# A four-layer graph network on one core: the preparation and the end of the hyperbolic layers rewritten in a fixed order

## Chip, core and metric

The kernel runs on one core of a Trainium2 chip. The metric is the device time of one execution in microseconds. Times of single instructions come from one profiled execution. The engines are TensorE (PE), VectorE (DVE), ScalarE (ACT), GpSimd (POOL) and SyncE (SP); SP issues nearly all large transfers, ScalarE and GpSimd issue some small ones from their own queues.

## What is computed

`x` is 3327 x 64, `adj` is a 3327 x 3327 matrix of zeros and ones with about 0.5% ones. Four layers follow each other; each normalizes its rows, applies a ReLU and adds its result to `x`:

```python
h = jnp.maximum(_layernorm(x, axis=-1), 0.0);  x = x + _L0_gnn_ref(h, adj, ...)   # hyperbolic attention, c = 1
h = jnp.maximum(_layernorm(x, axis=-1), 0.0);  x = x + _L1_gnn_ref(h, adj, ...)   # sum over the last 100 neighbours with decay
h = jnp.maximum(_layernorm(x, axis=-1), 0.0);  x = x + _L2_gnn_ref(h, adj, adj, ...)   # two GRU cells
h = jnp.maximum(_layernorm(x, axis=-1), 0.0);  x = x + _L3_gnn_ref(h, adj, ...)   # hyperbolic attention, c = 1 / r**2
```

The change concerns layers 0 and 3. Both compute, for all pairs of rows,

```python
adj_att = sigmoid(left + right.T) * adj            # left, right: products of logmap0(h) with two weight columns
x_local = _logmap(h[:, None, :], h[None, :, :], C)
support_t = einsum('ij,ijd->id', adj_att, x_local)
return _proj(_expmap(h, support_t, C), C)
```

Here `h` is the normalized row after the ReLU, called h' below; its squared length |h'|^2 enters nearly every factor.

## The kernel before

Rows are padded to 3328 = 26 tiles of 128. `X` holds all of x in SBUF as 128 partitions x 26 tiles x 64 numbers. A function `hyperbolic_series` does a hyperbolic layer; it is called for layer 0 (`r` is None, `masks` is None: adj is read from memory as f32) and for layer 3 (`masks` holds adj as fp8 in SBUF, and `done` stores each finished half). It has three stages.

**Preparation** (L361 to L479). `norm_relu` makes the means, `H`, its squares on ScalarE, their sums on VectorE, a root with one refinement step (`sqrt_`, L95 to L103), and writes the normalized rows back to `H`. Then H is squared and summed again for `x2` = |h'|^2. From `x2` come `ax` = x2 - 1, its inverse `ia`, and `Xr` = H x 2 ia. `Xr` is split into two f16 parts, `hi` and `lo`, in `Xp`. TensorE transposes Xp to columns (`to_columns16`, L410; the copies out of PSUM alternate between ScalarE and VectorE), multiplies these with the weights (`pw`), and VectorE makes `left` and `right` from that. `left` is brought to one row per tile, `LT`, and spread over the partitions as `leftB` by matmuls (L461). `Xe` holds the f16 rows with nine extra columns (from x0 = (x2 + 1) ia, split in three), is transposed to `XE`, and the first chunk's part to `XF`. `keep_busy` issues matmuls whose result is not used (L423). Here Tile's scheduler orders the instructions of each engine.

**Loop** (L482 to L630). The columns are cut in four chunks of 4, 3, 3 and 3 tiles per half. For each of 4 x 26 pairs of chunk and row tile: ScalarE makes `sig` (L517), POOL multiplies it with adj (L519), TensorE makes the products in a PSUM slot (L530, L531), ScalarE squares (`y`, L537), VectorE applies the series and multiplies with `sig` (L542, L543), TensorE sums (L552, L560). The order is written by hand. `load(k)` (L503) fetches adj for layer 0 into four buffers; its first four calls stand at the start of the loop, in the pool of the loop. The loop leaves `M`, `M0`, `hm` and `mm`.

**End** (L632 to L742). Some seventy VectorE instructions on 128 x 26 numbers, mostly each waiting for the one before, with Sqrt and Tanh on ScalarE, give two factors `ah` and `am` per row; then X gets Xr x ah + M x am (L739, L740), in halves in layer 3, in one piece in layer 0.

In layer 1, which follows the end of layer 0, ScalarE loads the weights `wt` (L1251, L1252) after POOL has cleared that tile (L1250); POOL issues the loads of other weights (L1213 to L1226) ahead of it. VectorE's first step of that layer is the mask (L1287).

Of the kernel before, what the change touches and what calls it, by code (L numbers as in the profile page):

```python
# [19 lines left out]
P = 128  # L20
# [26 lines left out]
def tile_gnn4(ctx: ExitStack, tc: tile.TileContext, x, adjT, att0, b0, w1, bias1, w_gat, a_gat,  # L47
# [46 lines left out]
    def sqrt_(pool, src, name):  # L94

        s0 = pool.tile(list(src.shape), F32, name=name)
        rc = pool.tile(list(src.shape), F32, name=name + "_r")
        A.activation(s0, src, AF.Sqrt)
        V.reciprocal(rc, s0)
        V.tensor_mul(rc, rc, src)  # L100
        V.tensor_add(s0, s0, rc)
        V.tensor_scalar(s0, s0, 0.5, None, op0=OP.mult)
        return s0  # L103
# [200 lines left out]
    def hyperbolic_series(r, params, ok, masks=None, done=None):  # L304
# [18 lines left out]
        with ExitStack() as st:  # L323
# [18 lines left out]
            px = st.enter_context(tc.tile_pool(name="hsx", bufs=2))  # L342
            XC, XF, leftB = {}, {}, {}
# [20 lines left out]
            with tc.tile_pool(name="hsp", bufs=1) as tp, tc.tile_pool(name="hsps", bufs=2, space=PSUM) as ps:  # L364
                A.memzero(X0)
                Xe = tp.tile([P, T, KE + 9], F16, name="Xe")
                E, Fe = Xe[:, :, D:KE], Xe[:, :, KE:]
                V.memset(E[:, :, 6:], SX)
                for k, part in enumerate(f16_parts((1.0 - 2.0 * G1) * SX)):
                    V.memset(Fe[:, :, 6 + k:7 + k], part)  # L370

                def parts3(x_, name, dtype):

                    o = tp.tile([P, T, 3], dtype, name=name)
                    lo = tp.tile([P, T], F32, name=name + "_r")
                    for k in range(3):
                        V.tensor_copy(o[:, :, k], x_ if k == 0 else lo)
                        if k < 2:
                            V.tensor_sub(lo, x_ if k == 0 else lo, o[:, :, k])
                    return o  # L380

                H = tp.tile([P, T, D], F32, name="H")
                norm_relu(tp, H)
                sq = tp.tile([P, T, D], F32, name="sq")
                for ts in HALVES:
                    A.activation(sq[:, ts, :], H[:, ts, :], AF.Square)
                for ts in HALVES:
                    V.reduce_sum(x2[:, ts], sq[:, ts, :], axis=AX.X)
                if r is not None:
                    V.tensor_scalar(x2, x2, cc, None, op0=OP.mult)  # L390
                ax = tp.tile([P, T], F32, name="ax")
                V.tensor_scalar(ax, x2, 1.0, None, op0=OP.subtract)
                V.reciprocal(ia, ax)
                ia2 = tp.tile([P, T], F32, name="ia2")
                V.tensor_scalar(ia2, ia, 2.0, None, op0=OP.mult)
                if r is not None:
                    V.tensor_scalar(ia2, ia2, sqc, None, op0=OP.mult)
                for ts in HALVES:
                    V.tensor_mul(Xr[:, ts, :], H[:, ts, :], wide(ia2[:, ts]))
                    A.activation(hi[:, ts, :], Xr[:, ts, :], AF.Copy, scale=SX)  # L400
                V.tensor_scalar(root, x2, 1.0, None, op0=OP.max)
                root_ = sqrt_(tp, root, "zs")
                table_of(AF.Sigmoid, root_[:, :1])
# [3 lines left out]
                def to_columns16(dst, src, rows, odd):  # L407
                    for t0 in range(0, T, 4):
# [6 lines left out]
                        else:  # L415
                            A.activation(dst[:, t0 * P:(t0 + n) * P], pt[:rows, :n * P], AF.Copy)

                junk = ps.tile([P, 512], F32, name="junk", bufs=1)
# [7 lines left out]
                to_columns16(XT, Xp[:, :, :2 * D], P, 1)  # L426
# [6 lines left out]
                A.activation(Xe[:, :, :D], Xr, AF.Copy, scale=SX)  # L433
                x0 = tp.tile([P, T], F32, name="x0")
                V.scalar_tensor_tensor(x0, x2, 1.0, ia, op0=OP.add, op1=OP.mult)
                x0s = tp.tile([P, T], F32, name="x0s")
                V.tensor_scalar(x0s, x0, SX, None, op0=OP.mult)
                p0 = parts3(x0s, "p0", F16)
                h0, hm0, m0, l0 = p0[:, :, 0:1], p0[:, :, 0:2], p0[:, :, 1:2], p0[:, :, 2:3]
                for k, src in ((0, h0.to_broadcast([P, T, 3])), (3, m0.to_broadcast([P, T, 2])), (5, l0)):  # L440
                    V.tensor_copy(E[:, :, k:k + src.shape[-1]], src)


                V.tensor_copy(root, root_)
                z = tp.tile([P, T], F32, name="z")
                V.reciprocal(z, root)
                V.tensor_mul(z, z, ax)
                V.tensor_scalar(z, z, 0.5 * ARTANH_CLIP / SX, isqc, op0=OP.mult, op1=OP.mult)
                lr = tp.tile([P, T, 2], F32, name="lr")
                V.reduce_sum(lr, pw[:, :6 * T].rearrange("p (t k i) -> p t k i", k=2, i=3), axis=AX.X)  # L450
                left = tp.tile([P, T], F32, name="left")
                V.tensor_mul(left, lr[:, :, 0], z)
                pe = ps.tile([P, W], F32, name="pe", bufs=1)
                PE.transpose(pe[:T, :P], left, ident)
                A.activation(LT, pe[:T, :P], AF.Copy)
                nc.sync.dma_start(left_row, LT)
                c = chunks[0]
                for o, to in ((0, junk), (1, pe)):
                    for i in range(c[1]):
                        t = o * HT + c[0] + i  # L460
                        PE.matmul(to[:, i * P:(i + 1) * P], ident[:T, t:t + 1].to_broadcast([T, P]), LT,  # L461
                                  start=True, stop=True)
                    A.activation(leftB[c][:, o, :], to[:, :c[1] * P], AF.Copy)
# [1105 lines left out]
```

## Time and profile before

| | us |
|---|---|
| median of 3 runs (lowest to highest) | 829.16 (827.92 to 830.69) |
| profiled execution | 831.17 |
| its span, first to last instruction | 829.5 |
| VectorE busy in the span | 721.5 (87%) |
| TensorE busy | 662.2 (80%) |
| ScalarE busy | 562.0 (68%) |
| POOL busy | 419.0 (51%) |

The layers lie in the span so: preparation of layer 0 to about 31 us, its loop to 266, its end to 284; layers 1 and 2 to 543; preparation of layer 3 to 569, its loop to 802, its end to 822, and the last store after that. A row of the timeline gives start, duration, engine, line, operation and tiles, and in brackets the idle time of the engine before it with what ended it. A row of the chain gives start and duration of a piece of the chain of work that ended last. A queue that issues transfers is written ACTq or SPq.

### The profile page before, as it was taken

To read this page: it belongs to the slowest core of one execution; us is meant where nothing else is said; L and a number is where in the kernel's file an instruction comes from. 1 tells how busy PE (TensorE), PEld (TensorE's weight loads), DVE (VectorE), ACT (ScalarE), POOL (GpSimd) and SP (SyncE) were. 2 spreads that over 40 slices of the span, in tenths; PEclk is the share of its full clock that TensorE was granted. 3 is DMA by queue.
4 is the path that set the end of the run, shared out by engine and by line. 5 is a ranking of instruction groups with operands and counts; after the bars stand their busy time and mean duration, and the time that the engine had idled before them with its cause. 6 is when DMAs were issued, how large, how long until landed. Compare 5 with 4: busy or idle time off the path is not lost.

```text
span 829.5 us, 11810 instructions
## 1 busy us (share of the span) xinstructions
PE 662.2 (80%) x4228; PEld 251.2 (30%) x4228; DVE 721.5 (87%) x1013; ACT 562.0 (68%) x684; POOL 419.0 (51%) x283
## 2 busy tenths in 40 slices
PE   0889999999896059989970997618999999998940
PEld 0422233333331024435430662204222333333310
DVE  7689999999997999999989946796999999999966
ACT  3878888888884167777761306448888888888850
POOL 2499989989985310002300000004787777787720
PEclk9999999999999569999995899958999999999985
DMA  2577766767662639999943630002001001000001
GB/s 42 167 235 227 204 204 191 238 182 204 190 191 66 225 126 339 349 347 333 338 170 126 220 113 1 0 0 48 1 2 35 1 1 35 0 2 1 0 4 44
DMA packets 56887, 107.86 MB, mean 130 GB/s; under 512 B 8305, under 2 KB 32817, under 8 KB 56817
## 3 DMA queue, kind: packets, MB, share of 16 engines
q1 hardware_dynamic: 51712, 106.68, 40.2%
q10 hardware_dynamic: 4656, 0.08, 0.3%
q8 instruction: 35, 0.57, 0.3%
q0 software_dynamic: 448, 0.24, 0.1%
q14 instruction: 36, 0.29, 0.1%
HBM read 103.73 MB, written 0.88 MB: 126 GB/s over the span
## 4 chain that ended last, share of the span: by engine, by line
DVE 65%; PE 14%; DMA 7%; ACT 6%; issue 5%; POOL 2%; ACTq 1%; DVEq 0%; POOLq 0%
DVE sig L543 22%; DVE slot L542 20%; DMA adj<-in 7%; DVE same L1207 5%; PE acc L1407 5%; DVE mask L1287 3%; POOL sig L519 2%; PE slot L552 2%; ACT y L537 1%; DVE deg L1426 1%; PE cnt L1294 1%; DVE X L740 1%; DVE prod L739 1%; PE slot L560 1%; DVE ln_v L123 1%
## 5 line engine op out<-in xcount | busy, mean ns | idle before, releaser
L537 ACT ACTIVATE y<-slot,shift_c 128x768 f32<-128x768 f32 (+1 forms) x208 | 197.6, 950 | 69.7 <-ACT sig L517 48.1
L543 DVE TENSOR_TENSOR sig<-slot,sig 128x768 f32<-128x768 f32 (+1 forms) x208 | 213.2, 1025 | 24.7 <-POOL sig L519 2.7
L542 DVE SCALAR_TENSOR_TENSOR slot<-y,slot 128x768 f32<-128x768 f32 (+1 forms) x208 | 212.1, 1020 | 9.0 <-ACT y L537 8.9
L519 POOL TENSOR_TENSOR sig<-adj,sig 128x768 f32<-128x768 f32 (+1 forms) x104 | 201.8, 1962 | 24.8 <-ACT sig L517 14.7
L517 ACT ACTIVATE sig<-leftB,right 128x768 f32<-128x768 f32 (+1 forms) x208 | 204.1, 981 | 0.2
L519 POOL TENSOR_TENSOR sig<-mask,sig 128x768 f32<-128x768 fp8e4 (+1 forms) x104 | 174.6, 1680 | 57.2 <-ACT sig L517 53.1
L552 PE MATMUL slot<-sig,Xr 128*64 128x384 f32 (+1 forms) x832 | 187.2, 538 | 18.3 <-DVE sig L543 18.3
L530 PE MATMUL slot<-XC,XT 128*128 128x384 f16 (+1 forms) x416 | 142.1, 342 | 5.0 <-DVE sig L543 3.3
L531 PE MATMUL slot<-XF,XE 73*128 73x384 f16 (+1 forms) x416 | 141.4, 340 | 0.0
L1300 ACT ACTIVATE w<-cnt,ebias 128x832 bf16<-128x832 f32 x104 | 93.8, 950 | 32.4 <-PE cnt L1294 32.4
L1207 DVE TENSOR_SCALAR_CACHE_REDUCE same<-adj 128x1664 bf16<-128x1664 f32 x52 | 97.7, 1880 | 3.5 <-DMA adj<-in 3.5
L560 PE MATMUL slot<-sig,X 128*32 128x384 f32 (+1 forms) x832 | 95.0, 529 | 0.0
L468 POOL COPY Xp<-Xe 128x234 f16<-128x234 f16 x2 | 0.8, 415 | 160.1 <-DVE XT L414 146.4
L552 PEld LDWEIGHTS slot<-sig,Xr 128*64 128x64 f32 x832 | 42.9, 135 | 123.9 <-DVE sig L543 85.2
L1294 PE MATMUL cnt<-mask,after 128*128 128x416 fp8e4 x208 | 54.8, 347 | 25.3 <-DVE mask L1287 22.6
L178 POOL TENSOR_TENSOR mask<-mask,offdiag 128x128 fp8e4<-128x128 fp8e4 x26 | 16.8, 666 | 105.4 <-PE cnt L1294 104.2
L530 PEld LDWEIGHTS <-XT 128*128 128x128 f16 x416 | 40.6, 98 | 94.7 <-issue 68.8
L1294 PE MATMUL cnt<-mask,rest 128*128 128x416 fp8e4 x208 | 55.0, 347 | 12.5 <-ACT w L1300 12.5
L1287 DVE TENSOR_SCALAR mask<-adj 128x1664 fp8e4<-128x1664 f32 x52 | 53.3, 1031 | 6.7 <-DMA adj<-in 6.6
L531 PEld LDWEIGHTS <-XE 73*128 73x128 f16 x416 | 40.7, 98 | 33.3 <-issue 9.3
L1311 PE MATMUL acc<-w,h 128*64 128x416 bf16 x416 | 47.2, 349 | 0.0
L1407 PE MATMUL acc<-mask,h 128*64 128x416 fp8e4 x416 | 38.3, 346 | 0.1
(293 smaller groups left out, 547.7 us busy)
## 6 DMA issues: line engine op xcount, KB each, us to landing
adj<-in SPq DMA_DIRECT2D x65, 832.0 KB, 6.9
adj<-in SPq DMA_DIRECT2D x78, 384.0 KB, 3.9
adj<-in SPq DMA_DIRECT2D x27, 512.0 KB, 4.7
leftB<-left SPq DMA_DIRECT2D x6, 384.0 KB, 3.9
XC<-XT SPq DMA_DIRECT2D x12, 96.0 KB, 3.0
X<-in SPq DMA_DIRECT2D x1, 832.0 KB, 4.5
out<-X SPq DMA_DIRECT2D x2, 416.0 KB, 2.4
XF<-XT SPq DMA_DIRECT2D x6, 96.0 KB, 2.7
```

Source lines behind the costliest of these rows:

```text
L517: A.activation(sig, leftB[c], AF.Sigmoid, bias=right[:, b:b + 1])
L519: G.tensor_tensor(sig, adj, sig, op=OP.mult)
L530: PE.matmul(L[:, o, :c[1] * P], XT[:, rows], XC[c][:, o, :], start=True, stop=False)
L531: PE.matmul(L[:, o, :c[1] * P], XE[:KE, rows], XF[c][:, o, :], start=False, stop=True)
L537: A.activation(ys[k], Ls[k][:, :, :c[1] * P], AF.Square, scale=-0.5 / SX ** 2, bias=shift_c)
L542: V.scalar_tensor_tensor(L, y, G3, L, op0=OP.add, op1=OP.mult)
L543: V.tensor_mul(sig, L, sig)
L552: PE.matmul(acc[c][o * D:(o + 1) * D, 0, :n], Xr[:, b, :], sigs[k][:, o, :], start=b == 0, stop=b == T - 1)
L560: PE.matmul(acc[c][q:q + 32, 1, :n], X0[:, b - 1 + i, :], w[:, o, :], start=b == 1, stop=b == T - 1, tile_position=(0, q))
L1207: V.tensor_scalar(same, adj, 0.0, 0.0, op0=OP.is_equal, op1=OP.add, accum_out=count)
L1294: PE.matmul(cnt[o][:, h, :BK], w, cols(k, o, h), start=w is after and steps[k][1] == T - 1, stop=True, skip_group_check=True)
L1300: A.activation(ws[k][:, o, :, :], cnt[o][:, :, :BK], AF.Exp, scale=-LN2, bias=ebias)
```

## The change

`norm_relu` is no longer called by `hyperbolic_series`. Its steps stand there, with these differences: the ReLU R of the centred rows is squared on ScalarE beside the squares for the variance, and x2 is the sum of R's squares divided by the variance, so that the normalized rows are never written; Xr is R times one factor. Roots come as inverse roots with one refinement step (`inverse_root`).

The preparation is under `manual_schedule`: instructions stand on their engines as written. Small steps are placed between the copies of `to_columns16`. The copy of Xr into Xe is taken from `hi` by VectorE instead of from Xr by ScalarE. `left` is spread by matmuls directly from its columns; LT is made afterwards, for the later chunks only. X0 and the constant columns are cleared by POOL.

X is loaded in two halves. The adj buffers are in the pool of the columns, and the first four `load` calls stand ahead of the preparation. Numbers that only depend on x2 (k, kb, bx, bk, bh, rr) are made once, at the end of the preparation. The end uses them, has fewer steps, loads the Sqrt table at the end of the loop in layer 3, works in halves in both layers, and has M's last half multiplied by am on ScalarE, in thirteen activations, into `extra`.

```diff
+    def inverse_root(pool, src, name, root=None):
+        s0 = pool.tile(list(src.shape), F32, name=name) if root is None else root
+        if root is None:
+            A.activation(s0, src, AF.Sqrt)
+        q = pool.tile(list(src.shape), F32, name=name + "_q")
+        V.reciprocal(s0, s0)
+        V.scalar_tensor_tensor(q, src, -0.5, s0, op0=OP.mult, op1=OP.mult)
+        V.tensor_mul(q, q, s0)
+        V.scalar_tensor_tensor(s0, q, 1.5, s0, op0=OP.add, op1=OP.mult)
+        return s0
...
+            if masks is None:
+                for k in range(4):
+                    load(k)
+            with tc.tile_pool(name="hsp", bufs=1) as tp, tc.tile_pool(name="hsps", bufs=2, space=PSUM) as ps, \
+                    tc.manual_schedule(engines={mybir.EngineType.Activation, mybir.EngineType.DVE,
+                                                mybir.EngineType.PE, mybir.EngineType.Pool}):
-                A.memzero(X0)
+                G.memset(X0, 0.0)
...
-                norm_relu(tp, H)
+                for ts in HALVES:
+                    V.tensor_sub(H[:, ts, :], X[:, ts, :], wide(mean[:, ts]))
+                    A.activation(sq[:, ts, :], H[:, ts, :], AF.Square)
+                for ts in HALVES:
+                    V.tensor_scalar(R[:, ts, :], H[:, ts, :], 0.0, None, op0=OP.max)
+                    A.activation(sr[:, ts, :], R[:, ts, :], AF.Square)
+                for ts in HALVES:
+                    V.reduce_sum(v[:, ts], sq[:, ts, :], axis=AX.X)
+                V.tensor_scalar(v, v, 1.0 / D, LN_EPS, op0=OP.mult, op1=OP.add)
+                sd = new("sd")
+                A.activation(sd, v, AF.Sqrt)
+                V.reciprocal(rv, v)
+                V.reduce_sum(x2[:, HALVES[0]], sr[:, HALVES[0], :], axis=AX.X)
+                sd = inverse_root(tp, v, "sd", sd)
+                V.reduce_sum(x2[:, HALVES[1]], sr[:, HALVES[1], :], axis=AX.X)
...
+                V.tensor_mul(x2, x2, rv)
...
+                to_columns16(XT, Xp[:, :, :2 * D], P, 1,
+                             (of_x0, of_e, of_f, lambda: V.tensor_copy(Xe[:, :, :D], hi), of_z))
...
-                PE.transpose(pe[:T, :P], left, ident)
-                A.activation(LT, pe[:T, :P], AF.Copy)
-                nc.sync.dma_start(left_row, LT)
...
+                def of_left():
+                    for o, to in ((0, junk), (1, pe)):
+                        for i in range(c[1]):
+                            t = o * HT + c[0] + i
+                            PE.matmul(to[:, i * P:(i + 1) * P], left[:, t:t + 1].to_broadcast([P, P]), ident,
+                                      start=True, stop=True)
+                    V.tensor_copy(leftB[c][:, 0, :], junk[:, :c[1] * P])
+                    A.activation(leftB[c][:, 1, :], pe[:, :c[1] * P], AF.Copy)
+
+                to_columns16(XE, Xe, KE + 9, 0, (lambda: None, of_left))
...
+                PE.transpose(pe[:T, :P], left, ident)
                 keep_busy(6)
+                A.activation(LT, pe[:T, :P], AF.Copy)
+                nc.sync.dma_start(left_row, LT)
...
+                if r is not None:
+                    table_of(AF.Sqrt)
...
+                for k in range(T // 2):
+                    t = last.start + k
+                    A.activation(extra[:, k, :], M[:, t, :], AF.Copy, scale=am[:, t:t + 1])
...
-        nc.sync.dma_start(X, x.rearrange("p (t d) -> p t d", d=D))
+        for ts in HALVES:
+            nc.sync.dma_start(X[:, ts, :], x.rearrange("p (t d) -> p t d", d=D)[:, ts, :])
```

The steps named in the order above: `of_x0` makes x0 and splits it in three (seven instructions), `of_e` and `of_f` write the extra columns of Xe (three each), `of_z` makes the factor of `left` and `right` (six).

## The prediction

> **What bounds the kernel now.** I read the chain that ended last first: it says which engine's time is the program's time.
>
> ```profile
> DVE 65%; PE 14%; DMA 7%; ACT 6%; issue 5%; POOL 2%; ACTq 1%; DVEq 0%; POOLq 0%
> ```
>
> VectorE (DVE) carries the two hyperbolic loops (31 to 264 and 571 to 799 us), which the change leaves alone. It edits four short stretches around them: head of layer 0 (0 to 51 us), end of layer 0 (266 to 284), head of layer 3 (543 to 572), end of layer 3 (802 to 822). So I read the chain in order of time in each. In the head of layer 0:
>
> ```profile
> 1.32 4.16 ACTq L280
> ...
> 9.31 0.91 ACT ln_sq L121
> ...
> 19.11 1.87 DVE Xr L399 x2
> ...
> 38.21 6.51 DMA adj<-in
> ...
> 46.11 1.08 issue
> ```
>
> The reader is to see that the first limit is not x: ScalarE's queue stands 4.16 us at the loads of `wc`, behind `dcol` (3328 elements of 4 bytes), and its first Square comes when that queue has been worked off, at 9.31. GpSimd (POOL) comes last at the end of this stretch. The timeline of the end of layer 0, on the three engines that matter:
>
> ```profile
> 279.82 0.23 POOL L1250 MEMSET wt<- 128x128 f32 x1
> 280.09 0.50 ACTq L1251 DMA_DIRECT2D wt<-in  x1
> 280.50 3.81 DVE L740 TENSOR_TENSOR X<-X,prod 128x1664 f32<-128x1664 f32 x2
> 280.63 0.61 ACTq L1252 DMA_DIRECT2D wt<-in  x1
> ```
>
> ScalarE is told at 280.09 to load `wt`, because POOL, busy issuing the weights' loads since 266.7, clears `wt` only then. And in the end of layer 3 a table load stands in the path:
>
> ```profile
> 804.76 1.28 ACT L98 ACT_TABLE_LOAD   x1 [2.89 <-DVE t L684]
> ```
>
> **What the Trainium skill says.** "ScalarE: Activation LUTs", What ACT_TABLE_LOAD costs, gives about 1283 ns a load; the trace shows the same 1.28. "VectorE: DVE Perf Modes", What auto-detection actually checks, gives one-source operations two f32 results a cycle and four of 16 bits if both tensors lie in SBUF, tensor_tensor one. The trace agrees for f32: the mask (L1287) takes 1.02 us for 1664 elements, a product (L739) 1.89; it shows no large 16-bit copy out of SBUF. "DMA: Bandwidth & Descriptors", Queues, rings and completion order, has each engine go round-robin between queue rows, so `dcol` shares with whatever the sync queue (SP) has in flight. The trace fits: few of its packets moved until X had landed. "TensorE: Matmul & The Clock Gate", What's actually happening, has the fast clock granted after a busy window of about 3.4 us. In layer 3 the granted clock rises to 1.00 at 564.0, 5.4 us after TensorE began at 558.56.
>
> **Part 1, norm and |h'|^2.** Counted from ScalarE's first Square to the first `Xr`. Before, layer 0: 9.31 to 19.03, 9.7 us. After: Square 0.92, two reduces 1.95, scale 0.22, reciprocal 0.33, reduce 0.97, four steps of the inverse root 0.87, reduce 0.97, then x2, ax, ia, root, ia2 1.09: 7.3. Saved 2.4. In layer 3 that Square waits for VectorE alone, which is also given the two maxima R before the reduces (832 f32 at half of 1.02, 1.0 together); counted from the mean's first reduce (542.96) Xr moves from 556.55 to about 555.0: saved 1.6. Its table load (1.28) comes after four Squares, beside a reduce.
>
> **Part 2, loads of adj at the start.** SP now issues X in halves and the first adj loads before everything else. Of the wait for adj, 2.0 us are gained at POOL: it starts 1.0 after the first sigmoid ended (33.44 against 32.44), and waits 1.04 before its fifth tile; the 6.51 us in the chain are mostly covered by POOL's own tiles. But three loads of 512 KB are in flight behind X while `dcol` wants the same engines, and `wc` waits behind `dcol`. At one element of `dcol` per 2 KB row (about 100 in 0.5 us on 16 engines, as the rows passed at 32 us), the queue is free not at 5.5 but at 9.4: 3.9 us later. If the loads don't disturb it: 0. I take 3.0. The clearing of X0 leaves ScalarE for POOL: 0.7 back; POOL has time for it and the constant columns, since its `ident_h` is first wanted at 21 us and was there at 10.4. First Square 11.6, Xr 18.9: nothing is left of the 2.4. Later in SP's queue the fifth adj load stands behind the transposed copies and `leftB`, which waits for the store of `left` to land. That is near 37 us; its buffer frees at about 38 anyway and the tile is wanted at 45, so nothing.
>
> **Part 3, the preparation in fixed order.** From Xr to the first sigmoid before: 12.3 us (19.03 to 31.29). After, VectorE gets, behind `lo` (at 3.9): of_x0, seven dependent steps at 0.22, 1.5; XT copy; of_e and of_f 0.7; XT copy; the Xe copy (two to four elements a cycle, 0.5 to 1.0; at worst one, 1.7); of_z 1.5; only then the sixth XT copy, about 9.2, where it stood at 6.9. TensorE's sums for `left` wait for it: `left` comes at 10.5 against 9.1. Saved: the trip through LT, 0.7. Added: ScalarE does two XE copies and LT (0.55, 0.55, 0.3) after leftB and ahead of the first sigmoid, and TensorE's eighteen remaining transposes follow the eight broadcasts (2.05 before; wider weights, 2.4). First sigmoid at about 15, products 16.2 against 13.6: +2.6 in each head. This is with the fast clock. TensorE now idles about 2 us before `left`, so the busy window may not come in time; the broadcasts and transposes at half clock add 2.0 (0.12 against 0.07 for a transpose in the trace). I count it as even odds for each head, so once. The ten small steps moved to the end of the preparation (1.6) lie in the 3.1 us in which VectorE waits for the first `y`: nothing. Should that cover go, 1.6 per head.
>
> **Part 4, end of layer 0.** Shorter arithmetic: 266 to first product 8.2 us instead of 11.0, and one of eight half products (0.97) goes to ScalarE as thirteen activations of 64 columns. But they stand behind the two `wt` loads, which wait for POOL's memset. VectorE is through with the rest at 280.0; ScalarE begins at 281.25, needs 13 x 0.2 (0.18 to 0.26, between the rows of 26 and 384 columns), ends at 283.9; last addition 0.97, mask at 284.85 against 284.34: +0.5 (-0.5 to +1.1), not -3.8. What is late next is `extra`.
>
> **Part 5, end of layer 3.** From `hm` to the first product before: 12.14. After: 1.63 to t (was 2.30), table loaded while VectorE still reduces (-1.28), one step more to tanh (+0.22), reciprocal beside tanh (-0.35), shorter tail after the last root (-0.8), rest -0.3: 9.0. So -3.1; the half product goes to ScalarE, which is free here: -1.0. Together -4.1 (-3.3 to -4.8); the store follows directly.
>
> **Sum.** Head 0: Xr -0.1, order +2.6, adj -2.0: +0.5. End 0: +0.5. Head 3: -1.6 + 2.6: +1.0. End 3: -4.1. Clock, once: +2.0. Total -0.1, with an allowance of -0.6 since the copies may run at their better bounds: **-0.7 us**. The profiled execution took 831.17 (span 829.5 and 1.7 around it), 2.0 above the median of the runs, 829.16; the difference taken from the median gives 828.5.
>
> **Rivals.** (1) *Faster*: `dcol` isn't held up (3.0 less) and the clock is up in both heads (2.0 less): -5.7, 823.5. For it: only X's rows shared with `dcol` in the trace, and the round robin may favour it. Against: 4.16 us of stall behind X alone. (2) *Slower*: TensorE stays at half clock to the end of both preparations. Place: from `left` to the first products. Price: broadcasts +2.0, 34 transposes +1.7, six junk matmuls at 0.43 instead of 0.25 +1.1, first products +0.9, up to 5.7 per head, in place of my 2.0 once: +9.3 at most. It decides above 2.3 us per head (-2.1 + 2 x 2.3 = +2.5); I value it at 4.0: +5.3 with the allowance, 834.5. For it: the idle stretch before `left`; against: six junk matmuls stand in the order before the products. (3) *It doesn't do what it says*: the loads begin early, but POOL was held by itself; then 2.0 less gain, 830.5, no change.
>
> **How the numbers follow.** 0.3% is 2.5 us, about what a measurement can tell from no change. Forecast and rival 3 together 0.50, all within it (826.7 to 831.6); rival 1, with half of its size counting too, 0.28; rival 2 0.22. Faster 0.28, same 0.50, slower 0.22. Range: -5.2 to +4.8 round the median, 824.0 to 834.0; it leaves out the outer parts of rivals 1 and 2, about 0.1 each.
>
> **What would show it.** ScalarE's first Square near 11.6 (9 says rival 1). The sixth XT copy about 9 us after Xr. POOL without a wait for adj in its first six tiles. `extra` starting right after the `wt` loads in the end of layer 0, and mask near 285, less what was gained ahead; beside the first product in layer 3. No table load in the path at 804. The granted clock between `left` and the first products tells forecast from rival 2. I am wrong in the mechanism if the end of layer 0 gets shorter by over 1 us, or if either head gets shorter by over 2.

## Result and the profile after

| | before | after |
|---|---|---|
| median of 20 runs each, us | 829.16 | 831.97 |
| lowest to highest | 827.54 to 831.02 | 829.93 to 833.34 |
| profiled execution (its span) | 831.17 (829.5) | 832.70 (831.0) |

After over before is 1.0030, with a 95% interval from 1.0022 to 1.0038: the changed kernel is slower by 1.8 to 3.2 us. The prediction's time was 0.7 us below the kernel before and its likeliest case was no change, so the sign was wrong; the range held the result.

I read the two traces at events that both have: the first `Xr` product, VectorE's first product sum (`slot`, "sum" below), its scaling of `hm` behind the loop, the first mask of layer 1, the first reduce of layer 3, the last X. Differences of start times give the stages:

| stage, us | before | after | difference |
|---|---|---|---|
| start to Xr, layer 0 | 19.03 | 18.03 | -1.00 |
| Xr to sum | 15.64 | 20.30 | +4.66 |
| loop: sum to hm | 231.26 | 230.94 | -0.32 |
| end: hm to mask | 18.41 | 18.44 | +0.03 |
| layers 1 and 2: mask to the first reduce | 258.62 | 256.55 | -2.07 |
| reduce to Xr, layer 3 | 13.59 | 11.84 | -1.75 |
| Xr to sum | 15.91 | 19.46 | +3.55 |
| loop: sum to hm | 229.72 | 230.35 | +0.63 |
| end: hm to the end of the last addition to X | 19.96 | 17.67 | -2.29 |
| sum of the differences | | | +1.44 |

Only the two stretches from Xr to sum are longer by much. Layers 1 and 2, which the change does not touch, took between 254.7 and 260.3 us in the executions profiled for this study, so their -2.07 is within what one execution differs from another. The two profiled executions are 1.5 us apart where the medians are 2.8 apart, for the same reason: medians decide on totals, stages on causes.

The chain that ended last in the kernel after, shares by engine:

```profile
DVE 52%; PE 19%; issue 11%; POOL 5%; DMA 5%; ACT 5%; DVEq 0%; ACTq 0%; POOLq 0%
```

TensorE has 19% where it had 14%, issue 11% for 5%. (Part of this is layer 1, which was not changed: the chain passes there through TensorE's `cnt` for 5% of the span, and for 1% before.) The same chain in order of time, start of the program to the first tiles of layer 0:

```profile
1.32 8.66 DMA wc<-in
...
10.86 0.91 ACT sq L411
...
18.03 1.03 DVE Xr L436
...
43.45 1.96 PE slot L604 x3
45.41 3.79 issue
49.20 1.12 ACT y L589
```

The reader is to see three things. Square still stands behind small loads, and later than before (10.86 for 9.31). The transfer of adj (6.51 us in the chain before) is gone. In its place, at 43 to 49 us, ScalarE's next `y` waits for TensorE, which is slow there.

The timeline of the end of layer 0:

```profile
281.96 0.22 POOL L1298 MEMSET wt<- 128x128 f32 x1
282.21 0.50 ACTq L1299 DMA_DIRECT2D wt<-in  x1
...
282.76 0.61 ACTq L1300 DMA_DIRECT2D wt<-in  x1
283.41 3.21 ACT L780 ACTIVATE extra<-M,am 128x64 f32<-128x64 f32 x13 [7.35 <-DVE prod L787]
...
286.65 1.03 DVE L788 TENSOR_TENSOR X<-X,extra 128x832 f32<-128x832 f32 x1 [3.06 <-ACT extra L780]
```

`extra` starts right behind the `wt` loads, as forecast, and VectorE waits 3.06 us for it. The timeline of the end of layer 3, around tanh:

```profile
809.50 0.22 ACT L733 ACTIVATE th<-t 128x26 f32<-128x26 f32 x1 [0.24 <-DVE t L732]
...
809.74 1.28 ACT L119 ACT_TABLE_LOAD   x1
811.03 0.20 ACT L119 ACTIVATE spare<-th 128x1 f32<-128x1 f32 x1
811.27 0.19 DVE L736 TENSOR_TENSOR th<-th,ti 128x26 f32<-128x26 f32 x1 [1.45 <-ACT spare L119]
```

The table load ahead of the first root is gone from the path, but a new one has come into it: VectorE does not go on when tanh is done (809.72), but after ScalarE has loaded the next table and run `spare`. And ScalarE's timeline at the end of the preparation of layer 0:

```profile
34.09 0.27 ACT L526 ACTIVATE LT<-pe 26x128 f32<-26x128 f32 x1 [0.32 <-PE pe L524]
36.09 1.15 ACT L569 ACTIVATE sig<-leftB,right 128x1024 f32<-128x1024 f32 x1 [1.74 <-DVE bh L538]
```

The first sigmoid reads leftB and `right`, both there, and yet waits 1.74 us for `bh`, the last of the ten small steps (1.73 in layer 3). Before, it starts without a wait:

```profile
31.29 1.15 ACT L517 ACTIVATE sig<-leftB,right 128x1024 f32<-128x1024 f32 x1
```

### The profile page after: what moved, and what is told of

The parts are those of the page before. It is cut to its first block, busy times and chain, and to the rows that moved or that the text cites. A ratio compares the mean times of both kernels' runs of the same rounds, so it can differ in the third digit from the quotient of the medians.

```text
span 831.0 us, 11827 instructions
## 1 busy us (share of the span) xinstructions
PE 667.1 (80%) x4228; PEld 255.9 (31%) x4228; DVE 721.5 (87%) x999; ACT 561.9 (68%) x707; POOL 417.9 (50%) x293
## 4 chain that ended last, share of the span: by engine, by line
DVE 52%; PE 19%; issue 11%; POOL 5%; DMA 5%; ACT 5%; DVEq 0%; ACTq 0%; POOLq 0%
DVE sig L595 18%; DVE slot L594 17%; PE cnt L1342 5%; POOL sig L571 5%; PE acc L1455 5%; DMA adj<-in 4%; PE acc L1359 3%; DVE same L1255 3%; DVE mask L1335 2%; PE slot L604 2%; ACT y L589 1%; DMA wc<-in 1%; DVE deg L1474 1%; DMA gb<-in 1%; PE slot L612 1%
```

## Experiments

The theory from the two traces: the loss is made between Xr and sum in both layers, by the fixed order, by TensorE at half speed, and by the ten small steps; the end of layer 3 keeps part of its gain behind a false wait; the end of layer 0 is held by `wt`. Rivals: the preparations are even and the new ends lose; the early loads cost more than they bring; part 3's operations and not their order are dear. All times below are medians; ratios are to the kernel before, measured beside it, with 95% intervals. Stages are read from one profiled execution of each kernel.

**The change in two halves.** *prep_only* has the old end in the changed kernel:

```diff
-                if r is not None:
-                    table_of(AF.Sqrt)
...
```

> The changed kernel with the old end in both layers, so parts 1 to 3 alone. The theory formed from the two traces (the loss is in the two preparations: TensorE at half speed while it makes leftB, and the first sigmoid held by the ten small steps): 4 to 5.5 us above the kernel before, about 834, with the first products of layer 0 and layer 3 where the changed kernel has them. Rival (the preparations are even, +1.5 together as my sum had them, and the loss comes from the new end): within 2 us of the kernel before.

836.41 us, ratio 1.0088 (1.0071 to 1.0104). *end_only* has the new end in the kernel before:

```diff
                 sigmoid(0)
+                V.reciprocal(small["rr"], root)
+                V.tensor_scalar(small["k"], ia, -0.25 * G0 / SX ** 2, None, op0=OP.mult)
...
+                if r is not None:
+                    table_of(AF.Sqrt)
...
```

> The old preparation with the new end in both layers (the small numbers it needs are made at the start of the loop, while VectorE waits for the first y). Theory from the traces: the end of layer 3 gains 2.3 us and not 4.1, the end of layer 0 nothing, so 1.8 to 2.8 us below the kernel before, about 826.9. My prediction's terms (-4.1 and +0.5): 3.6 below. Rival (the end gains nothing once the tanh wait is counted): within 1 us.

826.92 us, ratio 0.9970 (0.9960 to 0.9980). The halves have opposite signs and the preparation is the loser, even more than expected (+7, with an interval of nearly 3 us). The stages: Xr to sum 19.16 and 19.45 us in prep_only; hm to the last X 17.64 in end_only, for 19.96. The rival with a losing end falls. The halves add to +5.1 us, though, where the change is +2.8: prep_only is 4.4 above the changed kernel, and its old end explains 2.3 of that. Its profile has 2.4 more in layers 1 and 2, which no edit touches; why is open. end_only also makes its seven small numbers at the start of the loop, where VectorE waits for the first `y`: there they cost nothing (Xr to sum 15.70, before 15.64).

**The ten small steps.** *steps_free*:

```diff
-            small = {n: pers.tile([P, T], F32, name=n) for n in ("rr", "k", "kb", "bx", "bk", "bh")}
+            small = {n: pers.tile([P, T], F32, name=n) for n in ("rr", "k", "kb", "bx", "bk", "bh", "ax", "x0", "good")}
...
                 sigmoid(0)
+                V.tensor_copy(X0[:, :, 0], x0)
...
```

> The changed kernel with ax, x0 and good in the pool that stays, and the ten small steps behind the first sigmoid in the order, so that nothing of the preparation's pool is read late. Theory (the first sigmoid tile takes the memory of that pool and waits for its last reader, 1.74 us in layer 0 and 1.73 in layer 3): the sigmoid starts right behind LT, 1.7 earlier in each head; of that 1.2 to 3.5 us of the whole stay, since the first y then waits for products in layer 3. So 829 to 830.8. My prediction's reading (the steps lie where VectorE waits anyway): no difference to the changed kernel, 832.

830.76 us, ratio 1.0019 (1.0011 to 1.0026). ScalarE's timeline of that kernel:

```profile
33.52 1.13 ACT L559 ACTIVATE sig<-leftB,right 128x1024 f32<-128x1024 f32 x1
35.84 1.12 ACT L579 ACTIVATE y<-slot,shift_c 128x1024 f32<-128x1024 f32 x1 [1.19 <-PE slot L573]
```

The wait for `bh` is gone, so the sigmoid waited because its tile takes memory of the preparation's pool, whose last reader was `bh`: it reads `ax`. But the next limit is near: `y` now waits 1.19 us for the products, so of the 1.74 about 0.55 is left. Xr to sum is 18.78 and 19.32 us. The seven kernels of this study that have the changed preparation as it stands took 19.16 to 20.30 in layer 0 (average 19.56); in layer 3 three of them took 19.45 to 19.47 and four 20.63 to 20.67 (average 20.15), after TensorE's granted clock had read 0.50 for 3.4 us and for 6.8. In steps_free it read so for 3.4, so the gain up to sum is 0.4 or more in layer 0 and 0.1 in layer 3. More is won inside the loops (229.75 for 230.57 and 228.57 for 230.06, averages of six and seven): the early sigmoids shorten TensorE's first wait there from 1.8 or 1.9 us to 1.3, and its clock does not fall. In the whole it is 1.2 us, at the lower end of what I expected, and the interval overlaps that of the changed kernel; its profiled execution took 3.1 us more in layers 1 and 2 than that of the changed kernel. The cause of the wait is shown, its price in the whole only roughly.

**The product behind tanh.** *tanh_free*:

```diff
-                    V.tensor_mul(th, th, ti)
+                    tn = new("tn")
+                    V.tensor_mul(tn, th, ti)
+                    th = tn
```

> The changed kernel with the product behind tanh in the end of layer 3 written to a tile of its own instead of over th. Theory (that product overwrites th, which the early load of the square root's table reads through spare, so VectorE waits 1.45 us for the load): first product and last X 1.3 to 1.5 us earlier after hm, the whole 1.4 below the changed kernel, about 830.6. Rival (the root at the end waits for its table anyway): no difference.

830.00 us, ratio 1.0010 (1.0001 to 1.0019). The timeline:

```profile
808.08 0.23 ACT L733 ACTIVATE th<-t 128x26 f32<-128x26 f32 x1 [0.24 <-DVE t L732]
...
808.50 0.19 DVE L737 TENSOR_TENSOR tn<-th,ti 128x26 f32<-128x26 f32 x1
```

The product starts 0.42 after the start of tanh and not 1.77 after it; hm to the first product takes 9.22 us for 10.58. The wait was the order write-after-read: the product overwrote `th`, which `spare` reads only to be ordered behind tanh.

**TensorE's speed.** *warm*:

```diff
                 for t in range(T):
+                    if t == 20:
+                        keep_busy(7)
                     PE.matmul(pw[:, t * 6:(t + 1) * 6], ...
```

> The changed kernel with seven junk matmuls between the 20th and the 21st of the 26 sums for left, where TensorE stands idle for 1.9 (layer 0) and 2.1 us (layer 3) behind the sixth XT copy. Theory (that idle stretch is why the sixteen f32 matmuls of leftB run at about half speed, 3.2 to 3.9 us in layer 0 and 3.2 to 3.8 in layer 3): they take 2.3 us, products come 0.9 to 1.6 earlier in each head, the whole 1 to 3 below the changed kernel. Rival (the sixteen are slower because the weights are 128 rows and not 26, as the prediction's 2.4 against 2.05 half says): they stay above 3 us and nothing moves.

828.24 us, ratio 0.9987 (0.9980 to 0.9994): 3.7 below the changed kernel, more than expected. TensorE's timeline in the changed kernel, and then in warm (in brackets the idle time before, and what ended it):

```profile
27.04 0.32 PE L500 MATMUL pw<-wlr,XT 128*128 128x6 bf16 x6 [1.86 <-DVE XT L480]
...
28.08 2.02 PE L513 MATMUL junk<-ident,left 128*128 128x128 f32 x8
29.89 1.91 PE L513 MATMUL pe<-ident,left 128*128 128x128 f32 x8
```

```profile
24.84 1.72 PE L491 MATMUL junk<-Xp,ident_h 128*128 128x512 f16 x7
...
27.91 1.16 PE L515 MATMUL junk<-ident,left 128*128 128x128 f32 x8 [0.15 <-DVE left L505]
28.91 1.06 PE L515 MATMUL pe<-ident,left 128*128 128x128 f32 x8
```

And the old form, in the kernel before:

```profile
28.53 1.15 PE L461 MATMUL junk<-LT,ident 26*128 26x128 f32 x8
29.52 1.05 PE L461 MATMUL pe<-LT,ident 26*128 26x128 f32 x8
```

Eight matmuls of leftB take 2.02 and 1.91 us after an idle stretch of 1.86, and 1.16 and 1.06 without it. The old form, with 26 rows of weights, took 1.15 and 1.05: the wider weights cost nothing, it is speed alone. The record of the granted clock says the same, though not in the kernel after, where it has nothing ahead of 32.53 us, which a window shows as 1.00. Here is that stretch in tanh_free, which has the same preparation, and then in warm (after the seconds: sum, PE, PEld, DVE, ACT, POOL, then the granted clock):

```profile
27.00:30.30 3.30, 3.22 (x24) 3.23 (x25) 1.32 (x7) 0.59 (x1) 0.00 (x0) 0.50 0.54 113
```

```profile
27.00:30.00 3.00, 2.85 (x34) 2.69 (x35) 1.86 (x6) 0.59 (x2) 0.00 (x0) 1.00 0.59 125
```

Xr to sum: 18.15 and 18.22, 1.4 and 1.9 less than the averages (in layer 3 it is 1.2 or 2.4, by which of the two values one compares with).

**The order.** *order*:

```diff
                 to_columns16(XT, Xp[:, :, :2 * D], P, 1,
-                             (of_x0, of_e, of_f, lambda: V.tensor_copy(Xe[:, :, :D], hi), of_z))
+                             (of_z,))
+                A.activation(Xe[:, :, :D], hi, AF.Copy)
...
-                to_columns16(XE, Xe, KE + 9, 0, (lambda: None, of_left))
+                of_left()
+                to_columns16(XE, Xe, KE + 9, 0)
```

> The changed kernel with another fixed order in the preparation: of_z alone ahead of the XT copies, the Xe copy on ScalarE, leftB's matmuls ahead of all XE transposes, of_x0, of_e and of_f on VectorE behind right. Theory (what VectorE does ahead of the sixth XT copy costs the 2.6 us that I gave the fixed order): left about 1.3 earlier (Xr + 8.5), products 1.5 to 2.5 earlier in each head, the whole 2 to 4 below the changed kernel. Rival (the order costs little; half speed and the ten small steps hold everything): products less than 0.7 earlier, the whole within 1 us of the changed kernel.

825.84 us, ratio 0.9963 (0.9949 to 0.9976): 6.1 below the changed kernel. The steps of_x0, of_e and of_f stand behind `right`, ahead of the copies of leftB. left comes 7.4 us after Xr (9.7 in the changed kernel), leftB's matmuls run at full speed as in warm, since TensorE stands idle for 0.63 us only, and Xr to sum is 16.87 and 16.80. The step from warm to order, 1.3 and 1.4 us per head, is the order itself without its effect on TensorE's speed.

**The early adj loads.** *adj_late* moved the four `load` calls:

```diff
-            if masks is None:
-                for k in range(4):
-                    load(k)
...
+                if masks is None:
+                    for k in range(4):
+                        load(k)
                 sigmoid(0)
```

> The changed kernel with its first four adj loads back at the start of the loop of layer 0. My prediction's terms: the loads hold dcol and so wc and the first Square; without them Square comes 2 to 3 us earlier (near 9), Xr as much, and GpSimd waits for adj in its first tiles again, +2.0. What the trace after says: first Square at 10.86 and bcol and cc behind wc at 8.66, so 1 to 1.5 earlier; and since the loop gained only 0.3 from the loads in place of 2.0, the whole is 0.5 to 1.5 below the changed kernel. Rival (the early loads carry their gain): 0.5 to 2 above it.

831.96 us, ratio 1.0035 (1.0022 to 1.0048): the changed kernel again, and no evidence. SyncE's order is not fixed by the text; its adj loads started at 1.72 us as in the changed kernel. What lets them start early is the pool of the tiles. *adj_back* puts them into the loop's pool (`wk`), and moves the calls there too:

```diff
-                adjs[k] = px.tile([P, 2, W], F32, name="adj", bufs=4)[:, :, :c[1] * P]
+                adjs[k] = wks[0].tile([P, 2, W], F32, name="adj", bufs=4)[:, :, :c[1] * P]
...
+                wks.append(wk)
+                if masks is None:
+                    for k in range(4):
+                        load(k)
                 sigmoid(0)
```

> The changed kernel with the adj tiles back in the pool of the loop, so that the first four adj loads start after the preparation again (moving the four calls alone, as adj_late did, left the program's order of loads as it was). The prediction's terms: Square comes 2 to 3 us earlier, GpSimd waits 2.0 for adj in its first tiles. The trace after: the first Square stands behind bcol and cc, which wait for earlier loads to land; if these are the adj loads' doing, Square comes at 9.3 to 9.5, Xr 1.3 earlier. Forecast: Xr 1.3 earlier, loop of layer 0 longer by 0.5 to 2; the whole within 1 us of the changed kernel. Rival (the early loads are worth what part 2 says): 1.5 to 2.5 above it.

834.38 us, ratio 1.0065 (1.0051 to 1.0079): 2.4 above the changed kernel, so the rival was right. ScalarE's timeline and then the chain in order of time:

```profile
9.16 0.45 ACTq L306 DMA_DIRECT2D cc<-in  x1
9.66 1.68 ACT L409 ACTIVATE sq<-H 128x832 f32<-128x832 f32 x2 [1.01 <-DVE H L408]
```

```profile
33.90 0.16 DVE bh L536
...
34.20 3.94 DMA adj<-in
...
38.30 2.36 POOL sig L569
```

Square comes at 9.66 for 10.86 and Xr 1.06 earlier, but the adj loads, like the sigmoid, now wait for `bh`, and GpSimd waits for them to 38.2; the loop is 2.8 longer (233.74). By these two stages early loads are worth 1.7 net in this preparation, by the medians 2.4.

**ScalarE's queue.** *params_sp*:

```diff
+        q = nc.scalar if r is None else nc.sync
...
-                nc.scalar.dma_start(wc[o * D:(o + 1) * D, :], ...
+                q.dma_start(wc[o * D:(o + 1) * D, :], ...
```

> The changed kernel with layer 3's four small loads (wc, bcol, cc) issued by the sync engine instead of ScalarE. Theory (they and the landings that they wait for are all that holds ScalarE between its table load and the first Square): Square at about 8.8, when the first half of H is there, in place of 10.86; Xr of layer 0 1.8 to 2.0 earlier, the whole 1.5 to 2 below the changed kernel. Rival (Square waits for dcol or X and not for these): no difference. The four loads may delay what SP issues behind them; layer 3 needs them at 540 us only.

830.76 us, ratio 1.0022 (1.0008 to 1.0037). ScalarE's timeline:

```profile
8.83 1.83 ACT L412 ACTIVATE sq<-H 128x832 f32<-128x832 f32 x2 [0.18 <-DVE H L411]
```

Square is at 8.83, as expected. So `dcol` is not what it waits for in the kernel after: it waits for layer 3's small loads ahead of it in the queue, whose issue waits for earlier loads to land (the `DMA wc<-in` of the chain). The early adj loads make that wait: in adj_back, and in no_order (below), whose adj loads start at 6.86 us and not at 1.72, this queue is free at 9.6 and 9.3, and at 10.8 in the changed kernel. Xr gains 1.15 only, since VectorE's reduces then follow its maxima without a gap.

**The end of layer 0.** *wt_dve*:

```diff
-            G.memset(wt, 0.0)
+            V.memset(wt, 0.0)
```

> The changed kernel with wt cleared by VectorE instead of GpSimd, so that ScalarE's two wt loads needn't wait for GpSimd and the half product extra can start when am is there. Theory (extra is held by these loads): extra starts about 277.5, not 283.4, and is done before VectorE wants it; mask 15.4 us after hm in place of 18.44, 3.0 less; in the whole 3 us, or less if layer 1, which waits for adj at 340 GB/s, gives it back. Rival (ScalarE's half product is too slow to pay at all): less than 1 us in this stage.

829.17 us, ratio 1.0001 (0.9993 to 1.0009): 2.8 below the changed kernel. The timeline:

```profile
277.11 3.21 ACT L780 ACTIVATE extra<-M,am 128x64 f32<-128x64 f32 x13 [1.48 <-DVE am L773]
...
283.26 1.03 DVE L788 TENSOR_TENSOR X<-X,extra 128x832 f32<-128x832 f32 x1
284.32 1.03 DVE L1335 TENSOR_SCALAR mask<-adj 128x1664 fp8e4<-128x1664 f32 x1
```

`extra` is done at 280.3, three us before it is wanted; hm to mask takes 15.77. The gain stays in the whole.

**Part 1 alone.** *norm_only*:

```diff
-                norm_relu(tp, H)
...
-                    V.tensor_mul(Xr[:, ts, :], H[:, ts, :], wide(ia2[:, ts]))
+                    V.tensor_mul(Xr[:, ts, :], R[:, ts, :], wide(ia2[:, ts]))
```

> The kernel before with the new arithmetic from X to Xr alone (squares shared, |h'|^2 made beside the root), everything else as it was and ordered by the planner. Theory: from the mean to Xr 1.75 us less in layer 3, 1.0 less in layer 0, or more there since no small load stands ahead of Square as in the changed kernel (up to 2.4); behind Xr nothing changes; the whole 2 to 4 us below the kernel before, about 826. Rival (part 1 is only worth something in a fixed order, the planner loses it): within 1 us of the kernel before.

822.65 us, ratio 0.9925 (0.9910 to 0.9940): 6.4 below the kernel before, more than either theory gave. The stages show 2.9 in layer 0 (Xr at 16.14) and 2.05 in layer 3 (11.54); Xr to sum is 15.74 and 15.86, as before. That is all of the 5.0 between the two profiled executions (826.18 and 831.17); the other 1.4 of the medians I can't place.

**Everything but part 3, and part 3 without its order.** *no_order* is norm_only with the early loads and the new ends; *planner* is the changed kernel with one edit, after which Tile's scheduler (the planner) orders the preparation again:

```diff
-            with tc.tile_pool(name="hsp", bufs=1) as tp, tc.tile_pool(name="hsps", bufs=2, space=PSUM) as ps, \
-                    tc.manual_schedule(engines={mybir.EngineType.Activation, mybir.EngineType.DVE,
-                                                mybir.EngineType.PE, mybir.EngineType.Pool}):
+            with tc.tile_pool(name="hsp", bufs=1) as tp, tc.tile_pool(name="hsps", bufs=2, space=PSUM) as ps:
```

> Parts 1, 2, 4 and 5 without part 3: the old preparation behind Xr in the planner's order, with the new arithmetic up to Xr, the early adj loads and the new ends (the small numbers are made at the start of the loop, behind the first sigmoid). Theory (part 3 costs 3.9 us in layer 0 and 4.2 in layer 3 between Xr and VectorE's first product sum, against 15.7 and 15.9 before, and turns the change's sign): those 15.7 to 15.9 come back, Xr is as early as in norm_only or 1 later, and the whole is 7 to 9 us below the kernel before, 820 to 822. Rival (the early loads and the new ends bring nothing once the heads are early): 823 to 825, as norm_only or norm_only less the end of layer 3.

> The changed kernel with only the fixed order taken off its preparation: the same operations, ordered by the planner as in the kernel before. If the order alone costs the time: Xr to VectorE's first product sum 16 to 17 us in place of 19.6 and 20.2 (the average of the changed kernel and its variants with that preparation), the whole 5 to 7 below the changed kernel, 825 to 827. If the changed operations cost it (leftB's f32 matmuls with 128 rows, the copies on VectorE, the ten small steps at the end, the first sigmoid behind them): less than 2 below the changed kernel.

no_order 821.77 us, ratio 0.9901 (0.9885 to 0.9917); planner 825.69 us, ratio 0.9944 (0.9929 to 0.9959). With the same operations as the changed kernel, planner has Xr to sum at 15.73 and 15.55, as before the change: the whole loss between Xr and sum is the order with what it brings, half speed and the late sigmoid, and not what part 3 changed. VectorE's timeline shows one way in which the orders differ. First the changed kernel, `of_z` ahead of the sixth XT copy; then planner, the same steps:

```profile
25.54 0.19 DVE L112 SCALAR_TENSOR_TENSOR zs_q<-root,rr 128x26 f32<-128x26 f32 x1
25.76 0.19 DVE L113 TENSOR_TENSOR zs_q<-zs_q,rr 128x26 f32<-128x26 f32 x1
...
26.57 0.42 DVE L480 COPY XT<-pt 128x512 f16<-128x512 f16 x1
```

```profile
16.87 0.17 DVE L448 TENSOR_SCALAR x0s<-x 128x26 f32<-128x26 f32 x1
16.95 0.19 DVE L112 SCALAR_TENSOR_TENSOR zs_q<-root,rr 128x26 f32<-128x26 f32 x1
17.05 0.18 DVE L113 TENSOR_TENSOR sd_q<-sd_q,sd 128x26 f32<-128x26 f32 x1
17.14 0.19 DVE L449 CAST p<-x0s 128x26 f16<-128x26 f32 x1
17.23 0.18 DVE L113 TENSOR_TENSOR zs_q<-zs_q,rr 128x26 f32<-128x26 f32 x1
```

In the fixed order each step waits for the one before it, 0.22 us from start to start. The planner puts steps of three independent chains (`sd`, `zs`, `x0`) in turn, 0.09 from start to start, most of them ahead of Xr, where the chain of `sd` leaves gaps, and Xr is no later for it (17.88, after 18.03). How much of the loss this interleaving wins back no run tests alone: order, still fixed and not interleaved, got 2.7 and 3.3 us of planner's 3.8 and 4.6. no_order gained less than it might have in layer 3: Xr to sum was 17.52 there, since TensorE's six junk matmuls took 2.74 us at half speed (1.50 in the other kernels).

**The versions that beat both.** *best* is the changed kernel with order, steps_free, tanh_free, wt_dve and params_sp; *best2* is no_order with the last three.

> All at once on the changed kernel: the other order, the ten small steps behind the first sigmoid, the tanh product in a tile of its own, wt cleared by VectorE, layer 3's small loads on the sync engine. Sum of what the single runs gave against the changed kernel (832.0): order -6.1, tanh -1.4 (its stage), wt -2.7 (its stage), small loads -1.8, small steps -1 to -2 in addition to the order: 818 to 820. In the stages: Xr to the first product sum on VectorE 16.0 in both layers (16.8 in order), hm to mask 15.7, hm to the last X of layer 3 16.3. Rival (these gains overlap, the loop takes back what the preparation gives): 822 to 824.

> no_order with the three mends: the tanh product in a tile of its own, wt cleared by VectorE, layer 3's small loads on the sync engine. If stages add up: no_order less 1.4, less 2.7, less up to 1: 815 to 818. Rival (what is gained at the end of layer 0 and in Xr is waited for in the loads of adj): no more than 1.5 below no_order.

best 819.58 us, ratio 0.9885 (0.9870 to 0.9900); best2 816.16 us, ratio 0.9831 (0.9815 to 0.9847), 13 us below the kernel before. best is as expected in total (its profiled execution took 823.17), but its Xr to sum is 16.86 and 16.55, not 16.0: with the sigmoid free, the products come 14.5 and 14.2 us after Xr, and they are the limit. best2 has Xr at 15.99, Xr to sum 15.71 and 16.00, hm to mask 16.00, hm to the last X 16.64.

## Why the prediction was wrong, point by point

Four terms of the sum failed: the ten small steps, put at nothing (they hold the first sigmoid by 1.7 us in each head); half speed, counted once (it came in both heads, 3.3 us in place of 2.0); the waits for adj, booked at -2.0 (the loop gave -0.3); and the end of layer 3, booked at -4.1 (it gave -2.3, as a table load came into the path behind tanh).

- **Part 1** (layer 0 saved 2.4 between Square and Xr, layer 3 saved 1.6 from the mean): right. 7.17 us for 9.72, so 2.55; and 1.75.
- **Part 2, the loads ahead of Square** (3.0 late; Square 11.6, Xr 18.9): too dear, and the mechanism was another. Square came at 10.86, Xr at 18.03. ACT's queue left its first `wc` loads at 6.44, and at 6.48 in adj_back, which has no early adj loads: they did not hold up `dcol` at all, where I had 3.0 (before, it was 6.13). What they delayed was the second set of small loads, by 1.2 us (adj_back); without that set ahead of it Square comes 2.0 earlier (params_sp).
- **Part 2, the waits for adj** (-2.0): GpSimd's waits for adj are gone, but the loop got 0.3 shorter only. The step that failed was to book a wait as time won without asking what comes next. Windows of the kernel before, then of the kernel after:

```profile
42.00:44.00 2.00, 2.00 (x10) 0.78 (x10) 1.44 (x3) 1.11 (x2) 1.82 (x1) 1.00 0.97 316
44.00:46.00 2.00, 1.55 (x8) 0.20 (x4) 2.00 (x2) 2.00 (x4) 1.14 (x1) 1.00 0.67 196
```


```profile
42.00:44.00 2.00, 0.62 (x4) 0.29 (x4) 1.90 (x3) 2.00 (x3) 2.00 (x2) 0.69 0.75 235
44.00:46.00 2.00, 2.00 (x8) 0.20 (x8) 1.90 (x3) 1.40 (x2) 2.00 (x3) 0.50 0.80 240
```

  TensorE's clock reads 0.50 from 42.8 to 49.6 us; the sums and products take nearly twice as long, and ScalarE stands idle for 3.8 us ahead of a `y`. Four kernels with early loads kept the clock in this loop (steps_free, order, no_order, best2): 229.75 to 230.37 us, 0.9 to 1.5 less than before. Five with the changed preparation (prep_only, tanh_free, params_sp, wt_dve and the kernel after), whose clock fell for as long, took 230.5 to 230.9. So about 1.2 of the 2.0 came, and the fall took more than half of that back; single executions say no more (end_only, with late loads, took 230.46). The fall followed idle stretches of 1.88 and 1.38 us at the first two tiles, 1.25 and 1.39 before. Longer waits make it likelier and don't decide alone: see the last section. Rival 3 had this little gain, though not its way.
- **Part 3, the order** (+2.6 per head at full speed): the sixth XT copy came 8.5 us after Xr and not 9.2, left 9.7 and not 10.5, so the working was a little dear. At full speed (warm) the first products came 15.3 us after Xr in both layers (16.2), 1.9 and 1.7 later than before; the 13.6 that I compared with is layer 3's, layer 0 had 13.3. Up to sum warm is 2.5 and 2.3 above the kernel before. That this is near my 2.6 is luck: about 0.6 of it is the late sigmoid, which I had put at nothing. order shows 1.3 to 1.4 us for what stands ahead of left.
- **Part 3, half speed** ("even odds for each head, so once", +2.0): it came in both heads, 1.4 and 1.9 us by warm. Size right, number of times wrong. Rival 2 had named this place; its price of 4.0 per head was too high, as the junk matmuls ran at full speed again (1.50 us for six) and the last eighteen transposes nearly so (1.62).
- **Part 3, the ten small steps** ("lie in the 3.1 us in which VectorE waits for first `y`: nothing"): this step failed. I looked only at VectorE's own wait and not at who waits for the memory that the steps read. They cost 1.74 and 1.73 us of the first sigmoid; of this about half a microsecond shows up to sum, more in the loop, and 1.2 in the whole for both heads (steps_free). The sentence behind it, "Should that cover go, 1.6 per head", had the size of the wait.
- **Part 4** (+0.5): 0.0. First product 8.37 us after hm (8.2), `extra` 0.247 us for each of thirteen activations (0.2), started 14.1 after hm (15.3, since GpSimd was done with `wt` 1.2 earlier). "Not -3.8" was right; the 2.7 that it leaves behind are what wt_dve gets.
- **Part 5** (-3.1 and -1.0): -1.56 and -0.73. The term of 3.1 was right but for the wait of 1.45: with tanh_free hm to the first product is 9.22, 2.92 less than before. I had put "reciprocal beside tanh" into the sum without looking at what else reads `th`.
- **The sum**: against the forecast (-0.7) the two stretches from Xr to sum came out 1.6 us dearer (8.2 for 2 x 2.6 + 2.0 - 0.6), the end of layer 3 1.8, the loop of layer 0 1.7, that of layer 3 0.6; Xr was better by 0.9 and 0.15, the end of layer 0 by 0.5, layers 1 and 2 by 2.07: +1.4. Nothing that I measured explains the -2.07; it stays open whether any of it belongs to the change. The other 1.4 us up to the 2.8 of the medians are not in these two executions.

My test for a wrong mechanism (an end or a head shorter by more than the bounds) did not trip; the heads failed on the other side, for which I had set no such bound.

## What to carry to other kernels

An instruction moved to where its engine waits anyway is free only if nobody waits for the memory that it reads: ask who gets that memory next, above all where a pool ends, and ask the same before a result is written over an operand that another engine still reads. An order fixed by hand has to beat the planner's in the same stretch before it is worth having: here it cost 4 us per head with the same operations, by small steps that stood ahead of what TensorE waited for, and by the slow TensorE behind that wait. A wait taken away is worth what the next limit leaves of it, and here a part was lost to TensorE's speed, which falls behind its own short waits.

## What the runs showed of the hardware

- VectorE's small steps of 128 x 26 start 0.22 us apart if each needs the one before, and 0.09 to 0.10 apart if they don't. The Trainium skill's "VectorE: DVE Perf Modes", The DRAIN you can't avoid, says that the next operation does not start until the pipe is empty, and that one which isn't held starts earlier; these traces agree: dependent steps of 0.19 us never overlap, independent ones do.
- A short idle stretch was followed by half speed. In all sixteen heads of the kernels with the changed preparation's order as it stands or with steps_free's edit, TensorE stood idle for 1.84 to 2.13 us behind small matmuls of six columns; in fifteen the granted clock reads 0.50 next to it, for 3.4 or 6.8 us, and in the sixteenth, where that record is missing, eight matmuls of leftB took 2.02 us for 1.16. In the six heads of warm, order and best, where the stretch was 0.41 to 0.63, the clock stayed at 1.00. The Trainium skill's "TensorE: Matmul & The Clock Gate", What's actually happening, gives an idle window of about 3.4 us for the fall; in these runs a shorter gap did.
- Waits don't decide alone. At the start of the loops, a first stretch of 1.8 us or more was followed by a fall in 17 of 18 cases (in layer 0 of order the clock stayed up behind 1.87 and 1.38 us), one of 1.25 to 1.7 in 7 of 16.
- An f32 matmul with 128 rows of weights took no longer than one with 26 rows (1.16 and 1.15 us for eight at full speed).
- Thirteen activations of 128 x 64 took 3.21 us, 0.247 each: splitting a half product for ScalarE costs more than three times VectorE's 1.02 for the whole half, and pays only where ScalarE has the time.
